# Experts' token lists from 16-bit places laid out with the token tiles innermost, and a first expert that takes its tokens in two halves

## The chip, the cores and the metric

The kernel runs on one NeuronCore of one Trainium2 chip. The metric is the device time of one execution in microseconds (us); lower is better. Five engines share the work: TensorE (PE, with its weight loads shown apart as PEld), VectorE (DVE), ScalarE (ACT), GpSimd (POOL) and SyncE (SP, which only issues DMAs). Each engine executes its own instructions in the order in which the program lists them, and engines wait for each other by semaphores.

## The reference, cut to what matters

```python
h = layernorm(x) * (1 + ca) + sa                  # x: (8, 1024, 256)
x = x + ga * attention(h)                         # 16 heads of 64
h = layernorm(x) * (1 + cb) + sb
xf = h.reshape(-1, 256)                           # 8192 tokens
scores = softmax(xf @ router_w + router_b)        # 8 experts
G, idx = top_k(scores.T, 512)                     # each expert chooses 512 tokens
h1 = relu(einsum("ekh,ehf->ekf", xf[idx], w1) + b1)   # f: 1024
eo = einsum("ekf,efh->ekh", h1, w2) + b2
y = zeros.at[idx].add(eo * G)
x = x + gb * y
```

All tensors are float32. The change concerns only the part after the attention: how each expert's list of 512 token numbers is made from the scores, and the order of the first expert's work.

## The kernel before, in words

**Attention and rows.** The attention fills the first 3,200 us. For each tile of 128 tokens it leaves a row in DRAM (`rows_d`: the normalised token, its 8 scores and its gate), and `out_store` (L666) has POOL copy the 8 scores into `scores` (L671), which holds for each token of a tile (partition) the scores by place `[KT, E, C]`: KT = 4, E = 8 experts, C = 16, so 64 token tiles for each expert.

**Search.** Four transposes on PE (L981) turn `scores` so that a partition holds an expert and a c, and DVE copies the result to `sc` (L985). Fifteen rounds of counting (L991 to L1022) then find each expert's 512th score. Every round needs the one before it. Small tables are made on POOL beside it: counters (`iota`, L957) and their casts (L958), the masks `whole`, `whole_h` and `earlier` (L964 to L975), and `zeros` (L977). This part is not ordered by hand: a scheduler orders its instructions on each engine, together with the last tiles of the attention stage. From the threshold come a running count and a place in the list (0 to 511, or -1) for each chosen token: `slot` (L1055), split into `lo` (the place modulo 32, L1058) and `hi` (the place divided by 32, L1059), all int32 and of 512 elements per partition.

**Lists.** For an expert e, `entries(e)` (L1071) makes on DVE two one-hot tensors: `hot` says which of 32 values `lo` has (128x2048), and `at_hi` which of 16 values `hi` has (128x1024). `ids` holds `at_hi` times the tile's first token (`first`) and times the partition number (`part`). In the kernel before, the one-hot index is the innermost dimension of all three. `choose(e)` (L1091) multiplies them on PE: 64 pairs of a weight load of 32 columns of `hot` and a matmul over 32 columns of `ids`, spread over four column groups of the array. `gather(e)` (L1108) folds the result into 512 token numbers and has POOL issue four indirect DMAs (L1123), each of 128 rows.

**Expert.** `turn(e)` (L1130) transposes the four row tiles on PE and copies them out on DVE (L1139) to `xT`; `inner(e, f)` (L1143) is the first layer, 8 blocks of matmuls over 512 tokens, each followed by a ReLU on ACT (L1151); `outer(e, j)` (L1155) is the second layer for 128 tokens, with two DVE operations (L1164, L1165) and an indirect DMA on POOL that adds the rows to the output (L1168).

**Order.** From L1176 the order is written out by hand: the lists, the gather and the turn of expert 0, then for each expert its 8 `inner` blocks and 4 `outer` tiles. `entries(e+1)` is put before them, `choose(e+1)` and `gather(e+1)` after the fifth and sixth block, `turn(e+1)` after the third outer tile. Only the last expert takes its tokens in two halves of 256.

Of the kernel before, what the change touches and what calls it, by code (L numbers as in the profile page):

```python
# [28 lines left out]
F32 = mybir.dt.float32  # L29
BF16 = mybir.dt.bfloat16  # L30
F16 = mybir.dt.float16
I32 = mybir.dt.int32
AF = mybir.ActivationFunctionType
ALU = mybir.AluOpType
AX = mybir.AxisListType
# [3 lines left out]
P = 128  # L39
# [4 lines left out]
def adaln_block(  # L44
# [15 lines left out]
    nc = tc.nc  # L60
    B, S, D = x.shape
    H, _, _, N = w_qkv.shape
    E, _, F = w1.shape
    K = 512
    KC = D // P
# [4 lines left out]
    FC = F // P  # L70
    KT = K // P
# [7 lines left out]
    ident = const.tile([P, P], F32, name="ident")  # L79
# [88 lines left out]
    for i in range(NT // 2):  # L168
        t = work.tile([P, 2, D], F32, tag="p", name=f"x_first{i}", bufs=PB)
# [599 lines left out]
    with tc.manual_schedule():  # L769
# [21 lines left out]
        while g < 4 * NSU + LAG or steps:  # L791
# [19 lines left out]
            turn = gm == 3 and 0 <= u < NSU  # L811
# [75 lines left out]
        def turn(t):  # L887
            out_turn(ps_s, b, t, tag="s")
# [40 lines left out]

    rt = ctx.enter_context(tc.tile_pool(name="route", bufs=1))  # L930
    C = NTT // KT
    lo = rt.tile([P, KT, E, C], I32, name="lo")
    hi = rt.tile([P, KT, E, C], I32, name="hi")
    LO = 32
    HI = K // LO
    iota_lo = rt.tile([P, LO], F32, name="iota_lo")
    iota_hi = rt.tile([P, HI], F32, name="iota_hi")
    fold = rt.tile([P, LO], BF16, name="fold")
    part = rt.tile([P, 1], F32, name="part")
    first = rt.tile([P, KT, C], F32, name="first")  # L940
    b2_sb = rt.tile([P, E, D], F32, name="b2_sb")
    nc.sync.dma_start(
        b2_sb.rearrange("p e d -> p (e d)"),
# [3 lines left out]
    with tc.tile_pool(name="search", bufs=2) as se, tc.tile_pool(  # L947
        name="pos", bufs=1
    ) as po_, tc.tile_pool(name="se_ps", bufs=2, space=PSUM) as sps, tc.tile_pool(
        name="pos_ps", bufs=1, space=PSUM  # L950
    ) as pps:
        for dst, pattern, mult in (
            (iota_lo, [[1, LO]], 0), (iota_hi, [[1, HI]], 0), (part, [[0, 1]], 1),
            (first, [[P, KT], [P * KT, C]], 0),
        ):
            i = po_.tile(list(dst.shape), I32, name=f"i_{dst.name}")
            nc.gpsimd.iota(i, pattern=pattern, base=0, channel_multiplier=mult)  # L957
            nc.gpsimd.tensor_copy(dst, i)  # L958
        nc.vector.tensor_reduce(
            fold, ident.rearrange("p (g l) -> p l g", l=LO), AX.X, ALU.max  # L960
# [4 lines left out]
        for base, sign in ((0, 1), (C - 1, -1)):  # L965
            nc.gpsimd.affine_select(
                out=whole, in_=whole, pattern=[[-sign * C, E], [0, C]], base=base,
                channel_multiplier=sign, compare_op=ALU.is_ge, fill=0.0,
# [22 lines left out]
        for s in range(15):  # L991
            bit = 28 - 2 * s
            cnt = se.tile([P, 3], F16, tag="cnt", name=f"cnt{s}")
            for k in range(3):
# [3 lines left out]
                    op0=ALU.is_ge, op1=ALU.add, accum_out=cnt[:, k : k + 1],  # L998
# [3 lines left out]
            base = se.tile([P, 4], I32, tag="base", name=f"base{s}")  # L1002
# [9 lines left out]
            if bit >= 8:  # L1012
                nc.vector.scalar_tensor_tensor(
                    cand, num.to_broadcast([P, 4]), float(1 << bit), base,
                    op0=ALU.mult, op1=ALU.add,
# [35 lines left out]
        p_no = pps.tile([P, KT, P], F32, name="p_no")  # L1051
        for i in range(KT):
            nc.tensor.transpose(p_no[:, i, :], up[:, i * P : (i + 1) * P], ident)
        slot = po_.tile([P, KT, E, C], I32, name="slot")
        nc.vector.tensor_scalar_add(  # L1055
            slot, p_no.rearrange("p i (e c) -> p i e c", e=E), -1.0
        )
        nc.vector.tensor_single_scalar(lo, slot, LO - 1, op=ALU.bitwise_and)  # L1058
        nc.vector.tensor_single_scalar(  # L1059
            hi, slot, LO.bit_length() - 1, op=ALU.arith_shift_right  # L1060
        )

    ew = ctx.enter_context(tc.tile_pool(name="ework", bufs=2))
# [5 lines left out]
    chosen = {}  # L1069

    def entries(e):  # L1071


        hot = ew.tile([P, KT, C, LO], BF16, tag="hot", name=f"hot{e}")
        nc.vector.tensor_tensor(
            hot, iota_lo.unsqueeze(1).unsqueeze(1).to_broadcast([P, KT, C, LO]),
            lo[:, :, e, :].unsqueeze(3).to_broadcast([P, KT, C, LO]), ALU.is_equal,
        )
        at_hi = ew.tile([P, KT, C, HI], BF16, tag="at_hi", name=f"at_hi{e}")
        nc.vector.tensor_tensor(  # L1080
            at_hi, hi[:, :, e, :].unsqueeze(3).to_broadcast([P, KT, C, HI]),
            iota_hi.unsqueeze(1).unsqueeze(1).to_broadcast([P, KT, C, HI]), ALU.is_equal,
        )
        ids = ew.tile([P, KT, C, 2 * HI], BF16, tag="ids", name=f"ids{e}")
        nc.vector.tensor_tensor(
            ids[:, :, :, :HI], at_hi, first.unsqueeze(3).to_broadcast([P, KT, C, HI]), ALU.mult
        )
        nc.vector.tensor_scalar(ids[:, :, :, HI:], at_hi, part, None, op0=ALU.mult)
        chosen[e] = hot, ids

    def choose(e):  # L1091


        hot, ids = chosen[e]
        pi = ps_ids.tile([P, 2 * HI + KT], F32, tag="pi", name=f"pi{e}")
        for i in range(KT):
            for c_ in range(C):
                r = c_ % 4 * LO
                nc.tensor.matmul(
                    pi[r : r + LO, : 2 * HI], hot[:, i, c_, :], ids[:, i, c_, :],  # L1100
                    start=(i == 0 and c_ < 4), stop=(i == KT - 1 and c_ >= C - 4),
                    tile_position=(0, r),
                )
        parts = ew.tile([P, 2 * HI], BF16, tag="parts", name=f"parts{e}")
        nc.vector.tensor_copy(parts, pi[:, : 2 * HI])
        chosen[e] = parts, pi

    def gather(e):  # L1108

        parts, pi = chosen[e]  # L1110
        for g in range(4):
            r = g * LO
            for i in range(2):
                nc.tensor.matmul(
                    pi[r : r + LO, 2 * HI :], fold, parts[:, i * HI + g * KT : i * HI + (g + 1) * KT],
                    start=(i == 0), stop=(i == 1), tile_position=(0, r),
                )
        tok = ew.tile([P, KT], I32, tag="tok", name=f"tok{e}")
        nc.vector.tensor_copy(tok, pi[:, 2 * HI :])
        rows = []  # L1120
        for j in range(KT):
            row = ew.tile([P, WIDE], F32, tag=f"row{j}", name=f"erow{e}_{j}")
            nc.gpsimd.indirect_dma_start(  # L1123
                out=row, out_offset=None, in_=rows_d,
                in_offset=bass.IndirectOffsetOnAxis(ap=tok[:, j : j + 1], axis=0),
            )
            rows.append(row)
        chosen[e] = tok, rows

    def turn(e):  # L1130
        tok, rows = chosen[e]
        xT = ew.tile([P, KC, K], F32, tag="xT", name=f"xT{e}")
        for k in range(KC):
            px = ps_x.tile([P, K], F32, tag="px", name=f"px{e}_{k}")
            for j in range(KT):
                nc.tensor.transpose(
                    px[:, j * P : (j + 1) * P], rows[j][:, k * P : (k + 1) * P], ident
                )
            nc.vector.tensor_copy(xT[:, k, :], px)  # L1139
        h1 = ew.tile([P, FC, K], F32, tag="h1", name=f"h1_{e}")  # L1140
        chosen[e] = tok, rows, xT, h1

    def inner(e, f, t0=0, n=K):  # L1143
        tok, rows, xT, h1 = chosen[e]
        ph = ps_h.tile([P, n], F32, tag="ph", name=f"ph{e}_{f}_{t0}")
        for k in range(KC):
            nc.tensor.matmul(  # L1147
                ph, ex_w[e][0][:, k, f * P : (f + 1) * P], xT[:, k, t0 : t0 + n],
                start=(k == 0), stop=(k == KC - 1),
            )  # L1150
        nc.scalar.activation(  # L1151
            h1[:, f, t0 : t0 + n], ph, AF.Relu, bias=b1_sb[:, e, f : f + 1]
        )

    def outer(e, j):  # L1155
        tok, rows, xT, h1 = chosen[e]
        po = ps_o.tile([P, D], F32, tag="po", name=f"peo{e}_{j}")
        for f in range(FC):
            nc.tensor.matmul(
                po, h1[:, f, j * P : (j + 1) * P], ex_w[e][1][:, f, :],  # L1160
                start=(f == 0), stop=(f == FC - 1),
            )
        eo = ew.tile([P, D], F32, tag="eo", name=f"eo{e}_{j}", bufs=4)
        nc.vector.tensor_add(eo, po, b2_sb[:, e, :])  # L1164
        nc.vector.scalar_tensor_tensor(  # L1165
            eo, eo, rows[j][:, D + e : D + e + 1], rows[j][:, ROW:], op0=ALU.mult, op1=ALU.mult
        )
        nc.gpsimd.indirect_dma_start(  # L1168
            out=out_rows,
            out_offset=bass.IndirectOffsetOnAxis(ap=tok[:, j : j + 1], axis=0),  # L1170
            in_=eo, in_offset=None, compute_op=ALU.add,
        )
# [3 lines left out]
    with tc.manual_schedule():  # L1176
        entries(0)
        choose(0)
        gather(0)
        turn(0)  # L1180
        for e in range(E - 1):
            entries(e + 1)
            for f in range(FC):
                inner(e, f)
                if f == FC // 2:
                    choose(e + 1)
                if f == FC // 2 + 1:
                    gather(e + 1)
            for j in range(KT):
                outer(e, j)  # L1190
                if j == 2:
                    turn(e + 1)
            if e + 4 < E:
                load_expert(e + 4)
        for i in range(2):
            for f in range(FC):
                inner(E - 1, f, i * K // 2, K // 2)
            for j in range(KT // 2):
                outer(E - 1, i * KT // 2 + j)


# [29 lines left out]
```

## Time and profile before

| what | us |
|---|---|
| median of 3 runs (3545.62 to 3549.22) | 3546.07 |
| the profiled execution: its own time | 3549.73 |
| the profiled execution: its span | 3548.0 |
| attention, to the last score copies on POOL | 3231.7 |
| search, to the start of `slot` on DVE | 3231.7 to 3282.7 |
| list, gather and turn of expert 0, to its first matmul | 3282.7 to 3301.0 |
| eight experts and the last rows' output | 3301.0 to 3548.0 |

The page gives for each engine its busy time; the span begins with the first instruction. PEclk is the share of TensorE's clock that was granted. In a timeline a line has the start in us, the duration in us, the engine, the line, the operation, what it writes and reads with shapes, the count, and in brackets how long the engine stood idle before it and what ended that.

### The profile page before, as it was taken

To read this page: it belongs to the slowest core of one execution; us is meant where nothing else is said; L and a number is where in the kernel's file an instruction comes from. 1 tells how busy PE (TensorE), PEld (TensorE's weight loads), DVE (VectorE), ACT (ScalarE), POOL (GpSimd) and SP (SyncE) were. 2 spreads that over 40 slices of the span, in tenths; PEclk is the share of its full clock that TensorE was granted. 3 is DMA by queue.
4 is the path that set the end of the run, shared out by engine and by line. 5 is a ranking of instruction groups with operands and counts; after the bars stand their busy time and mean duration, and the time that the engine had idled before them with its cause. 6 is when DMAs were issued, how large, how long until landed. Compare 5 with 4: busy or idle time off the path is not lost. (4 is left out here: it accounts for less than half of the span.)

```text
span 3548.0 us, 54197 instructions
## 1 busy us (share of the span) xinstructions
PE 3434.0 (97%) x20631; PEld 1444.1 (41%) x20631; DVE 2863.3 (81%) x3611; ACT 2437.4 (69%) x2996; POOL 2657.8 (75%) x1533
## 2 busy tenths in 40 slices
PE   8999999999999999999999999999999999993898
PEld 3333333334433443334433443344433444432566
DVE  6888888888888888888888888888888888887332
ACT  5877877777777777777777777777777777760111
POOL 3788777978788888977788888977788888881233
PEclk9999999999999999999999999999999999996899
DMA  4011012011220113111211113011211112124342
GB/s 79 13 43 31 25 46 65 26 44 44 63 53 27 51 51 65 31 40 50 59 51 31 48 52 64 31 40 52 58 50 31 52 47 58 49 77 152 94 103 42
DMA packets 190136, 185.39 MB, mean 52 GB/s; under 512 B 49308, under 2 KB 167596, under 8 KB 189748
## 3 DMA queue, kind: packets, MB, share of 16 engines
q1 hardware_dynamic: 173916, 160.54, 16.6%
q0 software_dynamic: 7168, 12.72, 1.8%
q10 hardware_dynamic: 8792, 8.67, 0.8%
q8 instruction: 162, 2.65, 0.3%
q14 instruction: 98, 0.80, 0.1%
HBM read 127.06 MB, written 63.21 MB: 54 GB/s over the span
## 5 line engine op out<-in xcount | busy, mean ns | idle before, releaser
L466 POOL TENSOR_TENSOR acc<-acc,p 128x1024 f32<-128x1024 f32 x764 | 1811.8, 2371 | 350.8 <-ACT p L438 317.7
L382 ACT COPY p<-s 128x1024 f32<-128x1024 f32 x1024 | 994.8, 1019 | 401.6 <-PE s L373 384.1
L435 DVE TENSOR_TENSOR p<-p,less 128x1024 f32<-128x1024 f32 x1024 | 1206.2, 1209 | 28.2 <-PE less L432 25.7
L387 DVE TENSOR_TENSOR top<-top,s 128x1024 f32<-128x1024 f32 x768 | 936.7, 1220 | 269.0 <-ACT p L382 228.0
L438 ACT ACTIVATE p<-p 128x1024 f32<-128x1024 f32 x1024 | 1041.6, 1057 | 73.3 <-DVE p L435 73.0
L373 PE MATMUL s<-qk,qk 64*128 64x512 f32 x4096 | 1020.3, 611 | 15.4 <-DVE parts L413 12.3
L447 PE MATMUL av<-p,v 128*64 128x512 f32 x4096 | 969.1, 593 | 1.8 <-ACT oT L456 1.8
L373 PEld LDWEIGHTS s<-qk,qk 64*128 64x128 f32 x4096 | 359.2, 186 | 512.9 <-issue 223.0
L338 PE MATMUL pq<-hT,wq 128*64 128x512 f32 x2048 | 498.3, 608 | 2.2 <-ACT hT L303 2.2
L447 PEld LDWEIGHTS av<-p,v 128*64 128x64 f32 x4096 | 279.7, 137 | 456.4 <-issue 355.7
L463 POOL TENSOR_TENSOR acc<-p,p 128x1024 f32<-128x1024 f32 x128 | 304.2, 2377 | 163.0 <-ACT p L438 163.0
L338 PEld LDWEIGHTS pq<-hT,wq 128*64 128x64 f32 x2048 | 125.1, 136 | 341.6 <-issue 205.5
L355 PE MATMUL pv<-wq,hT 128*64 128x256 f32 x2048 | 249.2, 385 | 0.0
L1151 ACT ACTIVATE h<-ph,b_sb 128x512 f32<-128x512 f32 (+1 forms) x72 | 46.1, 640 | 255.2 <-PE ph L1147 255.2
L583 PE MATMUL po<-wo,ot 128*64 128x256 f32 x1792 | 205.7, 382 | 0.0
L355 PEld LDWEIGHTS pv<-wq,hT 128*64 128x64 f32 x2048 | 135.7, 136 | 152.3 <-issue 61.2
L405 DVE TENSOR_REDUCE tt<-tt 128x8 f32<-128x1024 f32 x112 | 137.7, 1230 | 56.4 <-PE tt L394 56.2
L387 DVE TENSOR_TENSOR top<-p,s 128x1024 f32<-128x1024 f32 x128 | 155.6, 1215 | 12.2 <-ACT p L382 12.2
L394 PEld LDWEIGHTS tt<-ident,top 128*128 128x128 f32 x1024 | 109.6, 140 | 109.8 <-DVE top L387 109.8
L528 POOL TENSOR_TENSOR oT<-oT,rb 128x1024 f32<-128x1024 f32 x63 | 151.0, 2397 | 0.0
L583 PEld LDWEIGHTS po<-wo,ot 128*64 128x64 f32 x1792 | 123.6, 137 | 66.1 <-issue 9.4
L394 PE MATMUL tt<-ident,top 128*128 128x128 f32 x1024 | 139.9, 280 | 4.7 <-DVE top L387 4.6
(185 smaller groups left out, 2291.5 us busy)
## 6 DMA issues: line engine op xcount, KB each, us to landing
rb<-rden_d SPq DMA_DIRECT2D x126, 256.0 KB
oT_d<-oT SPq DMA_DIRECT2D x62, 512.0 KB
ot<-oT_d SPq DMA_DIRECT2D x56, 512.0 KB
rows_d<-row SPq DMA_DIRECT2D x64, 132.0 KB
rows_d<-gb_d SPq DMA_DIRECT2D x8, 1024.0 KB
w<-in_L_ffn_w_dram ACTq DMA_DIRECT2D x8, 1024.0 KB
w<-in_L_ffn_w_dram SPq DMA_DIRECT2D x8, 1024.0 KB
lnx<-in_L_attn_inputs_dram SPq DMA_DIRECT2D x28, 256.0 KB
```

Of the source, the lines that this page charges most:

```text
L338: nc.tensor.matmul(pq[m * N : (m + 1) * N, :], wq_of(k, a, 2 * p + m), hTs[b][:, k, sl], start=(k == 0), stop=(k == KC - 1),)
L355: nc.tensor.matmul(pv[m * N : (m + 1) * N, i, :], hTs[b][:, k, t0 : t0 + N], wq_of(k, 2, 4 * g, 4), start=(k == 0), stop=(k == KC - 1),)
L373: nc.tensor.matmul(ps[:, j, :], kt[r, c * P : (c + 1) * P], qt[r, h * QB : (h + 1) * QB], start=True, stop=True,)
L382: nc.scalar.copy(probs[u, c], ps)
L387: nc.vector.tensor_tensor(tops[u], probs[u, 0] if c == 1 else tops[u], ps, ALU.max)
L394: nc.tensor.transpose(turned[u][:, 4 * j + t, :], top[:, j, t * P : (t + 1) * P], ident)
L435: nc.vector.tensor_tensor(probs[u, c], probs[u, c], less[u], ALU.add)
L438: nc.scalar.activation(probs[u, c], probs[u, c], AF.Exp)
L447: nc.tensor.matmul(avs[u][j * N : (j + 1) * N, :], v[:, c, hh * N : (hh + 1) * N], pT[:, j, :], start=(c == 0), stop=(c == NT - 1),)
L463: nc.gpsimd.tensor_tensor(sums[u], pts[0], pts[1], ALU.add)
L466: nc.gpsimd.tensor_tensor(sums[u], sums[u], pt, ALU.add)
L583: nc.tensor.matmul(po[m * N : (m + 1) * N, :], ot[:, p, m * N : (m + 1) * N], wo[:, p, :], start=(p == 0), stop=(p == NP - 1),)
```

## The change

- `slot`, `lo` and `hi` become int16, and the shift that makes `hi` a logical one.
- `iota_lo`, `iota_hi` and `first` are no longer rows of 32, 16 and 64 elements that are broadcast when they are read. They are spelled out once to 2048, 1024 and 1024 elements, the first two in int16, the last in bfloat16. POOL makes them as before, by an `iota` in int32 and a cast; the int32 tiles now share one buffer.
- `hot`, `at_hi` and `ids` have the 64 token tiles innermost and the one-hot index outside. A matmul of `choose` therefore reads 32 columns that lie 64 elements (128 bytes) apart.
- `entries` runs in the order `at_hi`, `ids` times `part`, `ids` times `first`, `hot`.
- `turn` and `inner` of expert 0 run in two halves of 256 tokens: the first half's `turn` needs two of the four gathered row tiles; the second half's comes after the fifth block of the first half. Its `choose(1)` and `gather(1)` lie in the second half.

```diff
-    lo = rt.tile([P, KT, E, C], I32, name="lo")
-    hi = rt.tile([P, KT, E, C], I32, name="hi")
+    lo = rt.tile([P, KT, E, C], I16, name="lo")
+    hi = rt.tile([P, KT, E, C], I16, name="hi")
...
-    iota_lo = rt.tile([P, LO], F32, name="iota_lo")
-    iota_hi = rt.tile([P, HI], F32, name="iota_hi")
+    iota_lo = rt.tile([P, LO, KT * C], I16, name="iota_lo")
+    iota_hi = rt.tile([P, HI, KT * C], I16, name="iota_hi")
+    first = rt.tile([P, HI, KT * C], BF16, name="first")
...
-    first = rt.tile([P, KT, C], F32, name="first")
...
         for dst, pattern, mult in (
-            (iota_lo, [[1, LO]], 0), (iota_hi, [[1, HI]], 0), (part, [[0, 1]], 1),
-            (first, [[P, KT], [P * KT, C]], 0),
+            (part, [[0, 1]], 1), (iota_hi, [[1, HI], [0, KT * C]], 0),
+            (first, [[0, HI], [P, KT], [P * KT, C]], 0), (iota_lo, [[1, LO], [0, KT * C]], 0),
         ):
-            i = po_.tile(list(dst.shape), I32, name=f"i_{dst.name}")
-            nc.gpsimd.iota(i, pattern=pattern, base=0, channel_multiplier=mult)
+            i = po_.tile(list(dst.shape), I32, tag="iota", name=f"i_{dst.name}")
+            to = i
+            if len(pattern) == 3:
+                to = i.rearrange("p h (t c) -> p h t c", t=KT)
+            nc.gpsimd.iota(to, pattern=pattern, base=0, channel_multiplier=mult)
             nc.gpsimd.tensor_copy(dst, i)
...
-        slot = po_.tile([P, KT, E, C], I32, name="slot")
+        slot = po_.tile([P, KT, E, C], I16, name="slot")
...
-            hi, slot, LO.bit_length() - 1, op=ALU.arith_shift_right
+            hi, slot, LO.bit_length() - 1, op=ALU.logical_shift_right
...
+        def of(x, n):
+            return x[:, :, e, :].unsqueeze(1).to_broadcast([P, n, KT, C])
+
+        def tiles(x):
+            return x.rearrange("p n (t c) -> p n t c", t=KT)
+
+        hot = ew.tile([P, LO, KT * C], BF16, tag="hot", name=f"hot{e}")
+        at_hi = ew.tile([P, HI, KT * C], BF16, tag="at_hi", name=f"at_hi{e}")
+        ids = ew.tile([P, 2 * HI, KT * C], BF16, tag="ids", name=f"ids{e}")
+        nc.vector.tensor_tensor(tiles(at_hi), of(hi, HI), tiles(iota_hi), ALU.is_equal)
+        nc.vector.tensor_scalar(ids[:, HI:, :], at_hi, part, None, op0=ALU.mult)
+        nc.vector.tensor_tensor(ids[:, :HI, :], at_hi, first, ALU.mult)
+        nc.vector.tensor_tensor(tiles(hot), of(lo, LO), tiles(iota_lo), ALU.is_equal)
...
-                    pi[r : r + LO, : 2 * HI], hot[:, i, c_, :], ids[:, i, c_, :],
+                    pi[r : r + LO, : 2 * HI], hot[:, :, i * C + c_], ids[:, :, i * C + c_],
...
-    def turn(e):
+    def turn(e, t0=0, n=K):
...
-            px = ps_x.tile([P, K], F32, tag="px", name=f"px{e}_{k}")
-            for j in range(KT):
+            px = ps_x.tile([P, n], F32, tag="px", name=f"px{e}_{k}_{t0}")
+            for j in range(n // P):
...
-            nc.vector.tensor_copy(xT[:, k, :], px)
+            nc.vector.tensor_copy(xT[:, k, t0 : t0 + n], px)
...
+        for e in range(E):
+            n = K // 2 if e in (0, E - 1) else K
+            if e == 0:
+                turn(0, 0, n)
+            if e + 1 < E:
+                entries(e + 1)
+            for t0 in range(0, K, n):
+                for f in range(FC):
+                    inner(e, f, t0, n)
+                    if e == 0 and t0 == 0 and f == FC // 2:
+                        turn(0, n, n)
+                    if t0 + n == K and e + 1 < E:
+                        if f == FC // 2:
+                            choose(e + 1)
+                        if f == FC // 2 + 1:
+                            gather(e + 1)
...
```

The scheduler orders the instructions of the search anew. On POOL, in program order, this is what stands between the score copies of the last-but-one pair of tiles and the gather of expert 0 (shapes in brackets where they are new):

```
before                              after
iota i_iota_lo                      iota i_part
iota i_iota_hi                      memset whole
iota i_part                         cast part
iota i_first                        memset earlier
memset whole                        iota i_iota_hi   (128x1024)
cast iota_lo                        affine_select whole
cast iota_hi                        cast iota_hi     (128x1024)
cast part                           affine_select whole
cast first                          iota i_first     (128x1024)
memset earlier                      cast whole_h
affine_select whole                 cast first       (128x1024)
affine_select earlier               affine_select earlier
affine_select whole                 iota i_iota_lo   (128x2048)
memset zeros                        copy scores (L671), last two tiles
cast whole_h                        multiply earlier
multiply earlier                    cast iota_lo     (128x2048)
copy scores (L671), last two tiles  memset zeros
```

More of the change, by code (lines that the diff above doesn't have):

```diff
@@ L32 @@
 I32 = mybir.dt.int32
+I16 = mybir.dt.int16
 AF = mybir.ActivationFunctionType
@@ L1071, in entries @@
     def entries(e):
[L1074 to L1088, printed above, removed]
+        def of(x, n):
[9 more added lines that the diff above has]
+        nc.vector.tensor_tensor(tiles(hot), of(lo, LO), tiles(iota_lo), ALU.is_equal)
         chosen[e] = hot, ids
@@ L1128, in gather @@
         chosen[e] = tok, rows
-    def turn(e):
-        tok, rows = chosen[e]
-        xT = ew.tile([P, KC, K], F32, tag="xT", name=f"xT{e}")
+    def turn(e, t0=0, n=K):
+        if t0 == 0:
+            xT = ew.tile([P, KC, K], F32, tag="xT", name=f"xT{e}")
+            h1 = ew.tile([P, FC, K], F32, tag="h1", name=f"h1_{e}")
+            chosen[e] += xT, h1
+        tok, rows, xT, h1 = chosen[e]
         for k in range(KC):
-            px = ps_x.tile([P, K], F32, tag="px", name=f"px{e}_{k}")
-            for j in range(KT):
+            px = ps_x.tile([P, n], F32, tag="px", name=f"px{e}_{k}_{t0}")
+            for j in range(n // P):
                 nc.tensor.transpose(
-                    px[:, j * P : (j + 1) * P], rows[j][:, k * P : (k + 1) * P], ident
-                )
-            nc.vector.tensor_copy(xT[:, k, :], px)
-        h1 = ew.tile([P, FC, K], F32, tag="h1", name=f"h1_{e}")
-        chosen[e] = tok, rows, xT, h1
+                    px[:, j * P : (j + 1) * P],
+                    rows[t0 // P + j][:, k * P : (k + 1) * P], ident,
+                )
+            nc.vector.tensor_copy(xT[:, k, t0 : t0 + n], px)
     def inner(e, f, t0=0, n=K):
@@ L1179, in adaln_block @@
         gather(0)
[L1180 to L1192, printed above, removed]
+        for e in range(E):
[14 more added lines that the diff above has]
+                            gather(e + 1)
+                if e == E - 1 or t0 + n == K:
+                    for j in range(t0 // P if e == E - 1 else 0, (t0 + n) // P):
+                        outer(e, j)
+                        if e + 1 < E and j == 2:
+                            turn(e + 1)
             if e + 4 < E:
                 load_expert(e + 4)
[L1195 to L1199, printed above, removed]
 _INS = [
```

## The prediction

> **What bounds the kernel now.** I read the busy time by stretches first, because the change touches only the end of the span. Its columns are the stretch, its length, busy time of PE, PEld, DVE, ACT and POOL, the granted clock, the DMA share and GB/s.
>
> ```profile
> 3200.00:3225.00 25.00, 21.34 (x206) 13.53 (x202) 16.59 (x51) 2.72 (x8) 12.30 (x28) 0.91 0.25 84
> 3250.00:3275.00 25.00, 1.48 (x9) 0.83 (x8) 22.60 (x94) 0.00 (x0) 0.00 (x0) 0.50 0.23 83
> 3275.00:3300.00 25.00, 5.48 (x86) 3.86 (x87) 13.15 (x21) 0.00 (x0) 4.11 (x4) 0.50 0.15 44
> 3350.00:3375.00 25.00, 25.00 (x162) 16.60 (x161) 10.15 (x16) 4.12 (x6) 7.03 (x5) 1.00 0.47 121
> ```
>
> The search (3232 to 3283) is a serial chain on DVE, with PE at half clock. From 3301 on PE is full: a DVE saving there is worth nothing, a longer PE instruction costs its whole length. Between them lies the list of expert 0, where nothing overlaps. The chain of waits holds only the last output row, so I followed waits by the timeline. First, how the search starts:
>
> ```profile
> 3230.70 0.71 DVE L664 TENSOR_SCALAR row<-ex,rd 128x8 f32<-128x8 f32 x2
> 3230.81 0.45 POOL L975 TENSOR_TENSOR earlier<-earlier,whole 128x128 f32<-128x128 f32 x1
> 3231.34 0.33 POOL L671 COPY scores<-row 128x8 f32<-128x8 f32 x2
> 3231.60 0.69 PE L981 MATMUL p_sc<-ident,scores 128*128 128x128 f32 x2 [1.26 <-POOL scores L671]
> 3232.32 0.69 DVE L985 COPY sc<-p_sc 128x512 f32<-128x512 f32 x1 [0.91 <-PE p_sc L981]
> ```
>
> POOL's copy of the last scores releases PE, PE releases DVE, and the search follows without slack. POOL had only just finished its tables. Then the list of expert 0:
>
> ```profile
> 3283.41 0.43 DVE L1058 TENSOR_SCALAR lo<-slot 128x512 int32<-128x512 int32 x1
> 3284.27 2.29 DVE L1075 TENSOR_TENSOR hot<-iota_lo,lo 128x2048 bf16<-128x2048 f32 x1
> 3286.48 1.22 DVE L1080 TENSOR_TENSOR at_hi<-hi,iota_hi 128x1024 bf16<-128x1024 int32 x1
> 3288.88 0.48 DVE L1088 TENSOR_SCALAR ids<-at_hi,part 128x1024 bf16<-128x1024 bf16 x1
> 3289.41 0.69 PE L1099 MATMUL pi<-ids,hot 128*32 128x32 bf16 x64 [6.77 <-DVE ids L1088]
> ...
> 3296.90 0.47 PE L1136 MATMUL px<-ident,erow 128*128 128x128 f32 x1 [0.99 <-DMA erow<-rows_d,tok]
> 3299.75 1.33 PE L1136 MATMUL px<-ident,erow 128*128 128x128 f32 x5 [0.98 <-DMA erow<-rows_d,tok]
> 3300.26 0.69 DVE L1139 COPY xT<-px 128x512 f32<-128x512 f32 x1 [9.38 <-PE px L1136]
> ```
>
> PE waits 6.77 us for DVE's lists, then for four gathered tiles, though two would start half an expert.
>
> [...]The trace has 2284 ns for `hot`[...]; no row shows the 16-bit rate. [...]the reduction to `fold` (L959) steps 128 bytes and takes 369 ns for 128 elements. L405 takes 1230 ns for 1024, so at the 1.04 ns per element below its fixed part is 165; (369 - 165)/128 is 1.59 ns, 1.53 times 1.04. [...]The two L664 take 0.71 us beside POOL's work, and their like at 3227.12 took 0.36 us with POOL idle.
>
> **Part A, POOL's tables (adds to the path).** In the changed program order thirteen POOL operations stand ahead of the last score copies, the spelled-out tables except the cast of `iota_lo` among them. Prices from the POOL groups: iota 134 ns for 1 element and 191 for 64, so 134 + 0.905n: 1.06 us for 1024, 1.99 for 2048. Casts 183 and 236 ns, so 183 + 0.841n: 1.04 us for 1024. Others as before: `part` 0.13 + 0.18, two memsets 0.20 each, masks 0.35, 0.34 and 0.29, `whole_h` 0.29. Sum 1.98 + two iotas 2.12 + two casts 2.08 + the last iota 1.99 = 8.17. Successive starts lie about 0.05 closer than durations (16 operations of 4.08 us before took 3.3), so 8.17 - 0.65 = 7.5 us from 3227.92: the copies start at 3235.4, not 3231.34. That is 4.1, and 0.1 more for L664[...]: **+4.2 us**. Nothing hides it, as DVE has only this search. Bounds: 3.8 (iota at the casts' slope) and 5.4 (at the steepest step, 32 to 64 elements, 1.09 ns, with 0.4 of blocking). What moved behind the copies (multiply, cast of 1.9 us, `zeros`) ends near 3238.7. It is first needed at 3275.8; the search's counting reads one tensor and writes its accumulator[...]. The SP queue keeps its order.
>
> **Part B, `lo`, `hi` and the lists of expert 0 (takes from the path).** Two-tensor rows: 1219 ns for 1024 and 2284 for 2048, so 154 + 1.04n; at two elements per cycle 0.69 and 1.22 us[...]. `lo` and `hi` (0.43, 0.42) to 0.29 if four per cycle. From the start of `lo`: before 3289.41 - 3283.41 = 6.0. After, as steps from start to start: 0.20 + 0.33 + `at_hi` 0.73 + `part` 0.34 + `first` 0.61 + `hot` 1.22 + 0.05 to PE = 3.5. **-2.5 us**. Bounds -2.7 and, if the broadcast rows keep the old rate, about 0. For the other seven lists DVE saves 2 us each beside a full PE: nothing, as the lists were ready 2.5 us before `choose` anyway (L1088 ends at 3338.96, L1099 starts at 3341.49).
>
> **Part C, two halves (takes from the path).** Row tile 1 lands at 3296.90; as before 0.51 us from the last row's transpose to the copy, then a copy of 256 columns at 0.43 (L1164's size) instead of 0.69, then 0.06: first matmul at 3297.90, not 3301.01, so -3.1. The second half's four transposes now lie in the full PE stretch: eight take 1.04, so +0.5. Rows 2 and 3 land by 3299.75, while PE is in the first block: no wait. Matmuls of 256 columns take half of 512 (the last expert: 32 in 6.9 us), ACT's ReLU 0.47 against 0.86 per block: free. PE's cold phase (4.2 us at half clock after its first matmul) moves along; its length can differ by 0.9 each way. **-2.6 us**, bounds -3.5 and -1.7. `gather(1)` comes 1.7 us nearer to `turn(1)`; from its first issue to that was 13.1 us, and gathers of expert 0 needed 8 to land: covered.
>
> **Part D, strided reads in `choose` (may add to the path).** Eight blocks of 64 pairs, all on PE's path. Now 0.60 us a block (3341.49 to 3342.09), 37 ns for a pair in each of four column groups. At half clock it took 0.69, so reading isn't what limits it. Below: 0. At 1.59 ns per column 32 take 51 ns: with loads beside matmuls 0.82 us, +0.2; one after the other 102 ns, 1.63 us, +1.0. I take +0.4, nearer the first because of the half-clock reading: **+3.2 us** for eight.
>
> Sum: 4.2 - 2.5 - 2.6 + 3.2 = +2.3 us. The profiled execution took 3549.73 (span 3548.0 and 1.7 around it), 3.7 over the median; in it this gives 3552.0. The runs' own spread is common to both kernels, so the median goes from 3546.07 to **3548.4**.
>
> **Rivals.**
> - *Strides are dear* (the other side): PE reads each column no faster than DVE and loads don't overlap matmuls, or worse. It decides from 1.0 us a block: 8.0 for 3.2 gives 3553.2 (+7.1); at twice that, 16 us, 3561. For: nothing in the trace reads so. Against: the small difference between half and full clock.
> - *POOL's large tables are slower than their slopes*: all slopes come from 64 elements or fewer. Twice the price adds 1.0 for each of four and 1.9 for the long iota, near +6: 3554. Against: the 512-element memset lies on the line (0.52 us, 128 take 0.20).
> - *The 16-bit rate isn't granted* (the edit doesn't do what it says): part B is 0: 3551.
> - *Strides are free and POOL's copies are less late* (2 us): 4.2 - 2 - 2.5 - 2.6 = -2.9: 3543.
>
> **How the numbers follow.** Chances: forecast (sum between -2 and +7) 0.61, dear strides 0.23, slow tables 0.07, no 16-bit rate 0.04, the last 0.05. About 0.2%, 7.1 us, is what a measurement of this kernel tells from no change. Even the best bounds, 3.8 - 2.7 - 3.5 + 0 = -2.4, stay inside; 0.03 is left for a faster result by something unseen. Over +7.1 lie the dear strides and part of the slow tables: 0.27. The rest, 0.70, is no change. The range is 3543 (best bounds) to 3558 (strides at 1.4 us a block): the dearer half of the stride case stays out above.
>
> **What would show it.** Right: L671's last copies near 3235.5 and the search moved whole; `hot` at 1.22 and `at_hi` at 0.69 us; the first L1147 about 0.8 us earlier than before (4.2 - 2.5 - 3.1 = -1.4, +0.6 for the first `choose` at half clock); L1099 at 0.8 to 1.0 us a block. Wrong: blocks over 1.6 us, iotas over 1.3, or copies not later than 3232.

## The result and the profile after

| | before | after |
|---|---|---|
| median, in one comparison of nine runs each | 3547.07 | 3557.61 |
| range of these runs | 3545.62 to 3549.22 | 3556.0 to 3559.71 |
| profiled execution, its own time | 3549.73 | 3556.13 |
| its span | 3548.0 | 3554.4 |

The ratio is 1.0028, with a 95% interval of 1.0020 to 1.0036: some 10 us slower (7 to 13). The forecast was 3548.4, the range 3543 to 3558; the time lies just under its upper end, among the times of the rival *strides are dear* (3553.2 to 3561).

The changed kernel's lines lie a little lower in the file: the score copies are at L672, the block of `choose` at L1103, `inner`'s matmul at L1153. The timeline of POOL in the changed kernel shows the tables ahead of the last score copies, in the order of its program:

```profile
3225.69 0.33 POOL L672 COPY scores<-row 128x8 f32<-128x8 f32 x2 [1.98 <-DVE row L665]
...
3226.70 1.03 POOL L962 IOTA i_iota_hi<- 128x1024 int32 x1
...
3228.00 1.04 POOL L963 CAST iota_hi<-i_iota_hi 128x1024 int16<-128x1024 int32 x1
...
3229.28 1.23 POOL L962 IOTA i_first<- 128x1024 int32 x1
...
3230.69 1.04 POOL L963 CAST first<-i_first 128x1024 bf16<-128x1024 int32 x1
...
3231.95 1.93 POOL L962 IOTA i_iota_lo<- 128x2048 int32 x1
3233.83 0.33 POOL L672 COPY scores<-row 128x8 f32<-128x8 f32 x2
```

From one pair of score copies to the next it is 8.14 us; before, it was 3.92 (3227.42 to 3231.34). The five large operations, 6.3 us together, make the difference: six small counters and casts of 1.1 us are gone, and the multiply and `zeros`, 1.0 us, have moved behind the copies. The last copies have no idle time ahead of them: POOL itself is what is late, and DVE's copy to `sc` now stands idle 4.28 us instead of 0.91.

The list of expert 0 and the start of its first half, in the changed kernel's timeline of all engines:

```profile
3285.88 0.29 DVE L1063 TENSOR_SCALAR lo<-slot 128x512 int16<-128x512 int16 x1
...
3286.41 0.69 DVE L1089 TENSOR_TENSOR at_hi<-hi,iota_hi 128x1024 bf16<-128x1024 int16 x1
...
3288.14 1.22 DVE L1092 TENSOR_TENSOR hot<-lo,iota_lo 128x2048 bf16<-128x2048 int16 x1
...
3289.50 1.87 PE L1103 MATMUL pi<-ids,hot 128*32 128x32 bf16 x64 [4.38 <-DVE hot L1092]
...
3291.41 0.19 DVE L1109 CAST parts<-pi 128x32 bf16<-128x32 f32 x1 [2.05 <-PE pi L1103]
...
3298.65 0.85 DVE L1147 COPY xT<-px 128x256 f32<-128x256 f32 x2 [6.55 <-PE px L1143]
...
3299.13 1.22 PE L1153 MATMUL ph<-xT,w 128*128 128x256 f32 x2
```

`hot` went from 2.29 to 1.22 us and `at_hi` from 1.22 to 0.69, but the 64 pairs of PE went from 0.69 to 1.87. In a stretch where PE is full, the block that makes the list of expert 2:

```profile
3340.56 1.92 PE L1103 MATMUL pi<-ids,hot 128*32 128x32 bf16 x64
3342.41 1.98 PE L1153 MATMUL ph<-xT,w 128*128 128x512 f32 x4
```

The kernel before, in the same view, has 0.66 for it:

```profile
3341.50 0.66 PE L1099 MATMUL pi<-ids,hot 128*32 128x32 bf16 x64
3342.09 1.12 PE L1147 MATMUL ph<-xT,w 128*128 128x512 f32 x2
```

The matmuls of `inner` behind it start 1.85 us after its start, against 0.59: nothing hides the difference. The two profiled executions stage by stage, each from start to start (`parts` is DVE's copy of what `choose` made):

| stage | before | after | difference |
|---|---|---|---|
| earlier score copies to last score copies | 3.92 | 8.14 | +4.22 |
| last score copies to `lo` | 52.07 | 52.05 | -0.02 |
| `lo` to first block of `choose` | 6.00 | 3.62 | -2.38 |
| that block to `parts` | 0.77 | 1.91 | +1.14 |
| `parts` to first `inner` matmul | 10.83 | 7.72 | -3.11 |
| first `inner` to first `outer` of expert 0, `choose(1)` within | 17.12 | 18.06 | +0.94 |
| from there to `parts` of expert 7: six periods, with a block of `choose` in each | 171.93 | 179.38 | +7.45 |
| the rest, with no `choose` | 57.94 | 57.83 | -0.11 |
| sum | | | +8.1 |

The two spans differ by only 6.4, as the attention stage ended 1.73 us earlier in this one execution. In the profiles of all kernels here the earlier score copies lie between 3225.7 and 3229.4, whatever the change, so this is the spread from one execution to the next, and I compare stages and not spans.

### The profile page after: what moved, and what is told of

Read it like the earlier page. It is cut to its first block, busy times and chain, and to the rows that moved or that the text cites. A ratio compares the mean times of both kernels' runs of the same rounds, so it can differ in the third digit from the quotient of the medians.

```text
span 3554.4 us, 54273 instructions
## 1 busy us (share of the span) xinstructions
PE 3440.4 (97%) x20663; PEld 1458.7 (41%) x20663; DVE 2846.2 (80%) x3613; ACT 2442.3 (69%) x3004; POOL 2664.3 (75%) x1533
```

## The experiments

Timed kernels of one comparison share their runs of the kernel before, whose median moved between comparisons (3547.07, 3548.32, 3549.23), so ratios are given.

**The change cut in two.** First the kernel before with only the two halves of expert 0:

```diff
-    def turn(e):
+    def turn(e, t0=0, n=K):
...
+            n = K // 2 if e in (0, E - 1) else K
```

> The kernel before with only the first expert in two halves (lists, tables and places as before). Theory: this part is a gain by itself, the first expert matmul comes 3.1 us earlier after the gather, four transposes (0.5 us) move into the full stretch: -2.6 us against before, 3544.5. Rival, that the halves lose: PE's cold phase, the second half's transposes or the copies behind the lists on VectorE cost what the early start gains: 0 to +2 us. The blocks of choose stay at 0.60 us under both.

Measured: 3546.19 in 13 runs, ratio 0.9993 (0.9985 to 1.0002), which alone can't be told from no change. Its profile can: `parts` to the first `inner` matmul took 7.81 us instead of 10.83, a gain of 3.02; 0.72 of it is given back before the first `outer`.

Then the changed kernel with the halves taken out:

```diff
-            n = K // 2 if e in (0, E - 1) else K
...
+        turn(0)
+        for e in range(E - 1):
+            entries(e + 1)
```

> The changed kernel without the halves: tables, places and layout of the change alone. Theory: the parts add up, tables +4.2, lists -2.4, eight blocks of choose +1.25 each, so about +12 us against before and +2.6 on the changed kernel: 3559 to 3560. Rival, that the halves are what loses in the changed kernel: 3555 or less.

Measured: 3560.86 in 6 runs, ratio 1.0034 (1.0022 to 1.0046). The times alone don't tell it from the change, as the intervals overlap; by its stages it is the slowest of the four combinations, +10.9 us against +8.1 for the change and -2.4 for the halves alone. Score copies to score copies 8.14, `lo` to `choose` 3.62, six periods 179.42: the tables and the layout carry all of the loss, and the halves give 2.8 us of it back.

**The tables behind the score copies.** In the changed kernel the tables are made after `sc`; a small copy that reads `sc` makes POOL wait for it.

```diff
+            if dst is part:
+                nc.gpsimd.tensor_copy(i, sc[:, :1])
             nc.gpsimd.iota(to, pattern=pattern, base=0, channel_multiplier=mult)
```

> The changed kernel with the spelled-out tables made on GpSimd behind the last score copies, during the search. Theory: the tables held up the score copies and with them the whole search by 4.2 us, so this takes 4.2 off the changed kernel: 3553.4; the last score copies start 0.3 us after VectorE's last row operation, the search is as long as before. Rival, that the delay was made up or is not on the path: 3557 to 3558. A second rival: the long casts beside the search block VectorE's small operations with two SBUF inputs[...], and the gain is 2 us or less.

Measured: 3555.36 in 21 runs, ratio 1.0021 (1.0014 to 1.0027). That is some 2.5 us under the 1.0028 of the change where 4.2 were expected, and the intervals overlap, so the stages have to tell. The distance between the score copies fell from 8.14 to 3.58, so the lateness was the tables' and all of it went. But the search grew from 50.34 to 51.67 us. DVE in this kernel's timeline:

```profile
3240.24 0.74 DVE L1003 TENSOR_SCALAR_CACHE_REDUCE above<-sc,cand 128x512 f32<-128x512 f32 x1
...
3240.91 1.57 DVE L1010 TENSOR_TENSOR base<-cand,steps_of 128x4 int32<-128x4 int32 x1
3242.41 0.15 DVE L1015 TENSOR_SCALAR_CACHE_REDUCE ge<-pc 128x3 f32<-128x3 f32 x1
...
3244.80 0.16 DVE L1010 TENSOR_TENSOR base<-cand,steps_of 128x4 int32<-128x4 int32 x1
```

and POOL at that moment:

```profile
3238.58 1.93 POOL L991 IOTA i_iota_lo<- 128x2048 int32 x1
3240.58 1.89 POOL L992 CAST iota_lo<-i_iota_lo 128x2048 int16<-128x2048 int32 x1
```

An addition of four elements, 0.16 us a round later, lasts until POOL's cast ends (3242.47). Two other small operations with two inputs, at 3235.78 and 3238.16, took 0.34 and 0.36 us and also ended with a cast. Not every pair does this: counting, with one tensor input, kept its 0.74 us beside the `iota` and the cast, and an operation with two inputs beside the `iota`, which reads nothing, kept its 0.16 (3238.71). It is the cost the prediction set at nothing because it looked at the counting alone; in the change itself POOL is done (3236.86) before DVE's first instruction of that kind (3238.08), so nothing was lost there. The rest of the shortfall lies after the first `inner` matmul: 19.47 us to the first `outer`, against 18.06 in the profile of the change. That is PE's cold phase, its time at half clock (0.50 of full) after the wait. The windows of the change (columns as in the stretches shown with the prediction) have the clock up from the second row on:

```profile
3299.00:3302.00 3.00, 2.91 (x8) 2.34 (x8) 2.96 (x6) 0.47 (x1) 0.00 (x0) 0.53 0.25 78
3302.00:3305.00 3.00, 3.00 (x16) 2.59 (x16) 0.36 (x1) 1.42 (x3) 0.00 (x0) 1.00 0.01 3
```

and those of the kernel with late tables one row later:

```profile
3298.00:3301.00 3.00, 2.91 (x7) 2.19 (x7) 2.96 (x6) 0.47 (x1) 0.00 (x0) 0.50 0.30 96
3301.00:3304.00 3.00, 3.00 (x9) 2.41 (x8) 0.53 (x1) 0.65 (x2) 0.00 (x0) 0.53 0.01 3
```

From the first `inner` matmul to full clock it was 2.7 us in the change's profile and 5.5 here, at half speed a difference of 1.4 us. The ten profiles in which the clock around this matmul was read finely lie between 2.7 and 5.5, and the changed kernel itself had 2.7 in one and 4.8 in another, so this part of the shortfall is no sign of the late tables. What sets it was not tried.

**Is it the distance of the columns?** The kernel before with the two halves, and with 16-bit places, but only two token tiles innermost, so that a `choose` reads columns 4 bytes apart. The tables are then of 64 and 32 elements.

```diff
+    iota_lo = rt.tile([P, LO, G], I16, name="iota_lo")
...
+        hot = ew.tile([P, M, LO, G], BF16, tag="hot", name=f"hot{e}")
+        at_hi = ew.tile([P, M, HI, G], BF16, tag="at_hi", name=f"at_hi{e}")
+        ids = ew.tile([P, M, 2 * HI, G], BF16, tag="ids", name=f"ids{e}")
```

with G = 2 and M = 64 / G.

> Two halves, 16-bit places, but the one-hot tensors have only two token tiles innermost, then the one-hot index, then the other tiles: the columns that a matmul of choose reads lie 4 bytes apart instead of 128, the tables have 64 and 32 elements. Theory[...]: blocks of choose back at 0.6 us, VectorE's lists still at 0.69 and 1.22 us, so -2.4 - 2.6 = -5 us against before: 3542. Rival (any step of more than one element costs PE the same): blocks at 1.8 us, 3552. Second rival (the places read in runs of two take VectorE's fast rate away): lists at 2.3 and 1.2 us, 3544.5.

Measured: 3544.41 in 21 runs, ratio 0.9988 (0.9981 to 0.9995): a little faster than the kernel before, and faster than the change. DVE's rate is that of the change, PE's block that of the kernel before:

```profile
3287.68 1.22 DVE L1094 TENSOR_TENSOR hot<-lo,iota_lo 128x2048 bf16<-128x2048 int16 x1
```

```profile
3338.55 0.66 PE L1105 MATMUL pi<-ids,hot 128*32 128x32 bf16 x64
3339.14 1.98 PE L1156 MATMUL ph<-xT,w 128*128 128x512 f32 x4
```

The score copies lie 4.17 us apart (+0.25), `lo` to `choose` takes 3.62, six periods 171.93 as before. The same with G = 4, 8 and 16 puts the columns 8, 16 and 32 bytes apart.

> As the kernel with two token tiles innermost, but with four: columns 8 bytes apart. [...]the block of 64 pairs takes half of 1.90, 0.95 us, and at least the 0.66 of the contiguous reads. Step theory (any step over some size costs in full): 0.66 or 1.90. Time against before as the kernel with two tiles innermost if the block is 0.66 (-4), else +2 more.

> As the kernel with two token tiles innermost, but with eight: columns 16 bytes apart[...]. [...]the block of 64 pairs takes the same 1.90 us as with 128 bytes. [...]If the cost comes only with larger steps: 0.66.

> As the kernel with two token tiles innermost, but with sixteen: columns 32 bytes apart. The block of 64 pairs took 0.66 us at 2 and 4 bytes, 0.74 at 8, 1.26 at 16 and 1.90 at 128. [...]if [...]the 1.90 comes from something else that large steps add[...], 1.26; if the cost grows with every doubling, 1.4 to 1.6.

The block, each from the timeline of its kernel. With 8 bytes:

```profile
3337.88 0.74 PE L1105 MATMUL pi<-ids,hot 128*32 128x32 bf16 x64
```

With 16 bytes:

```profile
3338.67 1.26 PE L1105 MATMUL pi<-ids,hot 128*32 128x32 bf16 x64
```

With 32 bytes:

```profile
3337.05 1.32 PE L1105 MATMUL pi<-ids,hot 128*32 128x32 bf16 x64
```

So 0.66 us at 2 and 4 bytes, 0.74 at 8, 1.26 at 16, 1.32 at 32 and 1.92 at 128. The stages agree: the six periods took 172.33 us at 8 bytes, 175.44 at 16, 175.70 at 32 and 179.38 at 128, against 171.93 before, for each block +0.07, +0.59, +0.63 and +1.24. The first rise lies between 8 and 16 bytes: a step of 8 bytes is nearly free here (+0.08), one of 16 adds 0.6, and one of 32 hardly more (+0.06 over 16). What makes the step of 16 bytes dear is not shown.

The expected sizes were missed: 0.95 at 8 bytes, which was the author's estimate, half of the 1.90 at 128 bytes, and at 16 bytes both 1.90 and 0.66. What the second rise, of 0.6 us from 32 to 128 bytes, comes from is not shown either. The kernel with 64 bytes gave no result, so whether it is a jump and where it lies stays open. The runs' times, one each, are in keeping: 3547.07 at 8 bytes and 3550.37 at 16 beside 3548.54 before, 3549.05 at 32 bytes beside 3546.44.

**The load or the matmul?** In the changed kernel, `ids` is written with its 32 columns side by side and only `hot` is read at 128 bytes, or the reverse.

```diff
-        ids = ew.tile([P, 2 * HI, KT * C], BF16, tag="ids", name=f"ids{e}")
+        ids_m = ew.tile([P, KT * C, 2 * HI], BF16, tag="ids", name=f"ids{e}")
+        ids = ids_m.rearrange("p m n -> p n m")
...
-                    pi[r : r + LO, : 2 * HI], hot[:, :, i * C + c_], ids[:, :, i * C + c_],
+                    pi[r : r + LO, : 2 * HI], hot[:, :, i * C + c_], ids[:, i * C + c_, :],
```

> The changed kernel, but only the weight loads of `choose` (`hot`) read columns 128 bytes apart; `ids` has its 32 columns side by side again, so the matmuls read as before the change. The block of 64 pairs took 0.66 us in full PE stretches with both side by side and 1.90 us with both 128 bytes apart. Theory one, both reads share one way into the array and add: about 1.28 us a block. Theory two, the load alone is what is slow: 1.90. Theory three, the matmul's read alone is slow: 0.66. Theory four, the two read beside each other and each alone is slow enough: 1.90 here and in the other run. The writes of `ids` now step 64 bytes on DVE, which can cost expert 0's list up to 1.2 us once.

> The changed kernel, but only the matmuls of `choose` (`ids`) read columns 128 bytes apart; `hot` has its 32 columns side by side again, so the weight loads read as before the change. Block of 64 pairs: theory one (reads add) about 1.28 us, theory two (the load is slow) 0.66, theory three (the matmul's read is slow) 1.90, theory four (beside each other, each slow enough) 1.90. The write of `hot` now steps 64 bytes on DVE: up to 1.2 us once for expert 0.

Measured with only the loads far apart:

```profile
3348.74 1.56 PE L1104 MATMUL pi<-ids,hot 128*32 128x32 bf16 x64 [1.14 <-DVE hot L1093]
```

and with only the matmuls' columns far apart:

```profile
3354.13 1.53 PE L1104 MATMUL pi<-ids,hot 128*32 128x32 bf16 x64 [3.24 <-DVE hot L1093]
```

Each alone adds about 0.9 us, both add 1.26. That is none of the theories whole: the reads don't add (that would be 2.4 for both), neither is the only slow one, and they overlap only in part: of the second 0.87 us some 0.5 are hidden. Reads wholly beside each other would take the longer of the two, 1.56, for both, and it was 1.92. To undo the loss both have to be brought together.

The times of these two kernels, 3571.59 and 3591.39 (3548.54 before), tell of something else that I had not expected: the bracket in both lines names DVE's `hot`, so that the list is late. DVE for expert 0, in the kernel in which `hot` is written 64 bytes apart:

```profile
3287.22 0.49 DVE L1091 TENSOR_SCALAR ids<-at_hi,part 128x1024 bf16<-128x1024 bf16 x1
3287.63 0.68 DVE L1092 TENSOR_TENSOR ids<-at_hi,first 128x1024 bf16<-128x1024 bf16 x1
3288.23 9.03 DVE L1093 TENSOR_TENSOR hot<-lo,iota_lo 128x2048 bf16<-128x2048 int16 x1
```

And in the other, in which `ids` is written 64 bytes apart:

```profile
3288.38 2.45 DVE L1091 TENSOR_SCALAR ids<-at_hi,part 128x1024 bf16<-128x1024 bf16 x1
3290.44 4.82 DVE L1092 TENSOR_TENSOR ids<-at_hi,first 128x1024 bf16<-128x1024 bf16 x1
```

The 9.03 us are 1.22, the 2.45 and 4.82 are 0.49 and 0.68 with the elements side by side. My bound for it, 1.2 us once, was far off, so these two runs are used for the length of the block alone.

**The change timed again.** The same kernel as the change.

> The changed kernel unaltered, timed anew with a larger number of runs beside the kernel before. The stages of the two profiled executions give +8.2 us (score copies +4.2, list of expert 0 -2.4, its block +1.1, first half -3.1, then +0.9 and six periods of +1.25), while the medians of the first timing differed by 10.5. If the stages hold everything, the ratio is 1.0023 here and its interval reaches under 1.0025; if something outside the routed part costs 2 us more, the ratio stays at 1.0028 to 1.0030 and the interval's lower end lies above 1.0024.

Measured: 3557.46 beside 3549.23, ratio 1.0025 (1.0015 to 1.0036). Neither reading is decided: the interval reaches under 1.0025, as the first asks, but holds both, and its middle lies between them. Its profile gives the same stages to within 0.02 us as far as `parts`, and 19.13 instead of 18.06 from the first `inner` to the first `outer`, with 4.8 us to full clock. Its sum, taken as above, is +9.5. Between +8.1 and +9.5 by stages and +8.2 to +10.5 by medians nothing of measurable size is left over.

## Why the prediction was right or wrong

- **The whole.** The forecast was +2.3 us with "no change" as the likeliest outcome; the kernel is 8 to 10.5 us slower, more than the 7.1 that the prediction counted as no change. What came is the rival *strides are dear*, which had a chance of 0.23. That the time still lies inside the range is luck in part: the upper end was to stand for 1.4 us more a block, but that makes +10.3 by the prediction's own terms, 3556.4, and 3558 would need 1.6.
- **Part A, right.** +4.2 was predicted, +4.22 measured; the search moved whole. The slopes from 64 elements and fewer held: 1.03 and 1.23 us for the `iota` of 1024 (1.06), 1.93 for 2048 (1.99), 1.04 for the casts (1.04). That the tables are the cause is shown by moving them: 4.56 us went, though 1.33 came back by a way that the prediction had argued off.
- **Part B, right.** -2.5 predicted, -2.38 measured; 1.22 and 0.69 us as priced, though one operand is still broadcast, and 0.29 and 0.28 for `lo` and `hi`. The price was an estimate, half of the 1.04 ns per element that float32 and int32 took; `hot` with its 16-bit inputs took (1.22 - 0.154)/2,048, 0.52 ns, beyond the same fixed part, and `lo` with 512 elements (0.29 - 0.165)/512, 0.24 ns. The rival that the rate isn't granted falls.
- **Part C, right.** The first matmul came 3.11 us earlier after the list (3.1 predicted) in the change, and 3.02 with the halves alone. What is given back before the first `outer` is 0.72 with the halves alone (0.5 predicted for four transposes). In the change's first profile nothing is: the +0.94 there is less than the 1.25 of the block, as PE was at half clock for 2.7 us and not the 4.4 of before (4.2 in the prediction); in its second profile, with 4.8, it was +2.01, 0.76 over the block. The cold phase was held to differ by up to 0.9 us each way and differed by more, though half speed halves what that costs. `gather(1)` stayed covered: the periods hold only the longer block.
- **Part D, the sign right and the size wrong.** This is the term that failed: "I take +0.4, nearer the first because of the half-clock reading", +3.2 for eight. A block cost 1.26 us more, the eight about 9.8 (1.14 + 1.25 + 7.45), some 6.6 over the term: that alone carries the forecast of +2.3 to 8.9, inside the measured 8 to 10.5. Two steps of its reasoning failed. One: because the block took 0.69 us at half clock and 0.60 at full, it was concluded that reading isn't what limits PE (0.60 is a distance between starts; its duration is 0.66). But the strided block, which is limited by its reads (only their step took it from 0.66 to 1.92), hardly depends on the clock either (1.87 at half, 1.92 at full), so the reading couldn't tell. Two: DVE's price of 1.59 ns per column, as no row of before had one for PE, was laid on four column groups that read at the same time. A block has 64 x 32 = 2,048 columns for the loads and as many for the matmuls. With one kind strided, 1.56 us is 0.76 ns per column if the groups read one after the other, and 3.0 ns if all four read at once; no run tells which, but 1.59 ns and four at once don't go together. The upper bound, "+1.0", came nearest by luck: it had loads and matmuls one after the other, which overlap in part, and too low a cost for each kind.
- The prediction priced a single step, 128 bytes, and took a value in the middle. The block's time depends on the step, 1.92 us at 128 bytes and 0.66 at the 4 bytes of two token tiles; that was the way out, and the prediction didn't look at it.
- **The other rivals.** Slow large tables fall by the 1.03 to 1.93 us; "strides free and copies less late" falls twice.

## What to carry to other kernels

A layout that helps the engine which writes a tensor has to be priced at the engine that reads it, above all if the reader is the one that is full: here 2 us of DVE per list were worth nothing beside a full PE (six periods took 171.93 us before and with two tiles innermost), and 1.26 us of PE per list counted in full. A step doesn't have to be all or nothing: two token tiles innermost already gave DVE its 16-bit rate (1.22 us for `hot`), left PE's block at 0.66 us, and shrank the tables from 2,048 elements to 64; with the halves, that kernel beats the one before by 0.12% (0.05 to 0.19). And where a scheduler may put set-up work ahead of the instruction that releases the critical chain, its length counts as latency (4.22 us here), but moving it behind let it collide with two-input DVE work there (an addition of 0.16 us took 1.57 beside a cast).

## What the hardware showed that was not expected

- PE's block of 64 pairs of 32 16-bit columns took 0.66 us at 2 and 4 bytes, 0.74 at 8, 1.26 at 16, 1.32 at 32 and 1.92 at 128: two rises, one between 8 and 16 bytes and one between 32 and 128.
- DVE's 16-bit results written 64 bytes apart took 9.03 us for 2,048 elements (1.22 side by side, 4.4 ns each), 4.82 for 1,024 (0.68), and a product with one tensor input 2.45 (0.49): five to seven times.
- An addition of four elements with two inputs took 1.57 us instead of 0.16 beside a POOL cast, and ended with it.
- From the first `inner` matmul PE needed from 2.7 to 5.5 us before its clock was full, 2.7 and 4.8 in two executions of the same kernel.
- With loads or matmuls alone at 128 bytes the block took 1.56 and 1.53 us, with both 1.92: the two reads neither add nor overlap wholly.
